# Grouped attention with half of its weights turned in VectorE blocks, values two groups behind, and the first scores of each group pinned in TensorE's order

## The chip, the cores and the metric

The kernel runs on one core of a Trainium2 chip. The metric is the device time of one execution in microseconds (us). Before the change three runs gave 2103.32, 2100.5 and 2106.19 us, so the median is 2103.32 us. All arithmetic is in float32. In the text, PE is TensorE, DVE is VectorE, ACT is ScalarE, POOL is GpSimd, and SP is the engine whose queue issues all DMAs of this kernel.

## What is computed

The reference runs four layers over an input of 8 sequences of 256 tokens with 512 features: a transformer block with rotary attention (8 query heads, one key head) and a gated MLP; a block with cosine attention over 16 heads and a GELU MLP; a grouped attention without MLP; and a layer of 8 small experts. Only the third layer's data path is rewritten by the change, and it computes, cut to what matters:

```python
B, T = 8, 256                     # 16 query heads of 32, 4 key/value heads
h = layernorm(x) * (1.0 + scale) + shift
q = h @ Wq.T                      # 16 heads
c_kv = h @ Wkd.T                  # a latent of 128
k, v = c_kv @ Wku.T, c_kv @ Wvu.T # 4 heads each
q, k = rotary(q), rotary(k)
scores = q @ k.T / sqrt(32)       # 4 query heads share a key head
scores = where(mask, -inf, scores) # window, global keys, no later block of 128
attn = softmax(scores)
x = x + (attn @ v) @ Wo.T
```

The mask hides the second block of 128 keys from the first 128 queries. So one head has 128x128 scores for its first query tile and 128x256 for its second, 384 columns in all.

## The kernel before

**The stages.** `run` (line 1835) calls them in order: attention of layer 0 ("attention0"), its MLP, attention of layer 1 ("attention1"), its MLP, attention of layer 2 ("attention2"), and the experts. The three attentions share one function, `attend` (line 653). By the trace attention2 runs from 1673.9 us to about 1951 us of the span.

**A tile scheduler sets the order.** The Python code lists instructions in program order, and a scheduler then orders each engine's queue: an instruction whose inputs are ready may be put ahead of earlier ones. `keep_in_program_order(ins)` forbids that for one instruction: it stays behind whatever was listed before it on its engine. On the chip each engine then works through its own queue strictly in order and waits on semaphores.

**Groups.** `attend` walks over 8 batches b and, in attention2, 4 groups g of 4 heads. One step of its loop does the following:

- `scored` (line 681): 16 PE passes per group write the scores of 4 heads into 4 PSUM banks "A" (line 693). The heads sit in different row groups of 32 of the array.
- `turned` (line 765) for the group before: PE transposes of the softmax weights, in 128x128 blocks, three per head in attention2, into a bank "C" (line 770), and then a copy back over the weights (lines 478 on DVE and 481 on ACT, by turns). Half of the heads are turned ahead of the softmax, the other half after a share of filler.
- `softmax` (line 699): for each head and query tile, DVE adds the mask and takes the minimum (line 731), then ACT takes the exponential and its sum (line 735). DVE then takes reciprocals of the sums (line 746) and turns them (line 750); two small DMAs through DRAM ("spread", lines 753 and 758) bring them back as a full tile.
- `some(quantum)`: a share of filler from a queue of generators, such as the next batch's projections (`project2`, line 634) and the output product of the batch before (`added`, line 1289). Both use line 629 on PE.
- `weighted` (line 777) and `divided` (line 807) for the group before: 16 PE passes (line 795) multiply the turned weights with the values, and DVE multiplies by the reciprocals (line 812).

**The other path for weights.** `in_blocks` (line 538) says how many of the four heads of a group avoid the PE transposes: two for batches 1 to 6 of attention0 and 0 to 6 of attention1, none in attention2. For such heads the scores and the mask are laid out in blocks, DVE transposes a whole tile of two heads in 32x32 blocks (line 740), four DMAs write it to DRAM ("flip", line 547, in `put`), and one DMA brings it back in place (line 744). Together this is a full transpose with no PE pass. In attention1 that tile is 128x1024.

**The next input.** `prepare` (line 517) normalises the input of batch b+2, transposes it on DVE (line 532) and writes it out in 4 DMAs ("turn", line 547); `fetch` (line 551) reads it back in 8 DMAs (line 565). `modulate` (line 581) then scales its four chunks of features, two on DVE (line 488) and two on ACT (line 489), all pinned in program order at the end of a batch. The first products of the next `project2` read these chunks one by one.

**Rotary part.** In `project2` DVE rotates queries and keys (lines 647 and 648), POOL adds the halves (lines 1651 and 1656), and PE transposes the result (lines 1237 and 1243), which `scored` needs for group 0 of the next batch.

**Buffers.** The pool "p" has 4 buffers for weights, "ctxT" has 4 for finished outputs, "row" has 3, and "wbig" has 8 tiles of 128x2048, of which attention2 uses three.

Of the kernel before, what the change touches and what calls it, by code (L numbers as in the profile page):

```python
# [34 lines left out]
P = 128  # L35
# [62 lines left out]
def constants():  # L98

    f32 = np.float32  # L100
    freqs = (f32(1.0) / f32(10000.0) ** (np.arange(0, 32, 2, dtype=f32) / f32(32))).astype(f32)
    ang = np.arange(S, dtype=f32)[:, None] * freqs[None, :]
    cos = np.cos(ang.astype(np.float64)).astype(f32)
    sin = np.sin(ang.astype(np.float64)).astype(f32)
    rope = np.stack([np.concatenate([cos, cos], 1), np.concatenate([-sin, sin], 1)], 1)
    rope = rope.reshape(TB, P, 2, 32).transpose(1, 0, 2, 3)
    i, k = np.arange(S)[:, None], np.arange(S)[None, :]
    hidden = ((np.abs(k - i) > 64) & (k % 64 != 0)) | (k // P > i // P)
    mask = np.where(hidden, f32(MASKED), f32(0.0))
    mask = np.concatenate([mask[:P, :P], mask[P:, :]], 1)  # L110
    return {
        "inv_freq": np.array([INV_FREQ], f32),
        "rope2": np.ascontiguousarray(rope),
        "mask2": np.ascontiguousarray(mask),
    }


# [61 lines left out]
class Program:  # L179
# [357 lines left out]

    def in_blocks(self, name, b):

        first = {"attention0": 1, "attention1": 0, "attention2": B}[name]  # L540
        return 2 if first <= b < B - 1 else 0

    def put(self, kept, tile):
# [107 lines left out]


    def attend(self, name, n_groups, hd, project, value, finish, work, key_tiles=(2, 2), biased=None,
               extra=None, then=None, spare=None, inverse=None, after=None):

# [23 lines left out]
        def scored(b, g):  # L681
            lhs_rhs = [got[b][0](g, j) for j in range(4)]
            s = [self.bank("A") for _ in range(4)]
            rows = P // hd
            for j0 in range(0, 4, rows):
                for q in range(TB):
                    for j in range(j0, j0 + rows):
                        lhsT, rhs = lhs_rhs[j]
                        keys = rhs(wide[q])
                        if j < self.in_blocks(name, b):  # L690

                            keys = keys.rearrange("p (k c i) -> p c k i", c=4, i=32)
                        nc.tensor.matmul(  # L693
                            s[j][:, at[q] : at[q] + wide[q]], lhsT(q), keys,
                            start=True, stop=True,
                        )
            return s

        def softmax(s, b):
            n_blocks = self.in_blocks(name, b)  # L700
            tot = self.t([P, 4, TB], "tot", 3)
            lows = self.t([P, 4, TB], "low", 3)

            blocks = self.t([P, 8 * P], "p")[:, : 2 * total]
            if n_blocks:
                put = blocks.rearrange("p (c h x) -> p h c x", c=4, h=2)
                ps = []
            else:
                ps = [blocks[:, j * total : (j + 1) * total] for j in range(2)]
            plain = self.t([P, 2, 512], "p")  # L710
            ps += [plain[:, j, :total] for j in range(2)]
            for j in range(4):
                low = lows[:, j, :]
                if biased is None:
                    nc.vector.tensor_reduce(
                        low, s[j].rearrange("p (q k) -> p q k", q=TB), AX.X, ALU.max, negate=True
                    )
                for q in range(TB):
                    cols = slice(at[q], at[q] + wide[q])
                    src, sign, out = s[j][:, cols], 1.0, None  # L720
                    if j >= n_blocks:
                        out = ps[j - n_blocks][:, cols]
                    else:
                        out = put[:, j, :, at[q] // 4 : (at[q] + wide[q]) // 4]
                        src = src.rearrange("p (c x) -> p c x", c=4)
                    if biased is not None:
                        by = biased[j < n_blocks][:, cols]
                        if j < n_blocks:
                            by = by.rearrange("p (c x) -> p c x", c=4)

                        nc.vector.tensor_tensor_reduce(  # L731
                            out, src, by, -1.0, BIG, ALU.add, ALU.min, low[:, q : q + 1]
                        )
                        src, sign = out, -1.0
                    nc.scalar.activation(  # L735
                        out, src, AF.Exp, bias=low[:, q : q + 1], scale=sign,
                        accum_out=tot[:, j, q : q + 1],
                    )
                if j == 3 and n_blocks:
                    nc.vector.transpose(blocks, blocks)  # L740
                    kept = self.flips[self.n_flip % 4][:, : 2 * total]
                    self.n_flip += 1
                    self.put(kept, blocks)
                    nc.sync.dma_start(blocks, kept)
            inv = self.inv[self.n_spread % 2]
            nc.vector.reciprocal(
                inv[:, 0 : 4 * TB].rearrange("p (j q) -> p j q", q=TB), tot
            )
            inv_t = self.t([P, 32], "invT", 2)
            nc.vector.transpose(inv_t, inv)  # L750

            kept = self.spread[self.n_spread % 4]
            nc.sync.dma_start(kept.rearrange("c (b r) -> b c r", b=4), inv_t)
            rows = kept.rearrange("(j q) t -> j (q t)", q=TB)
            by = []
            for c in range(nch):
                t = inverse[(self.n_spread * nch + c) % 4]
                nc.sync.dma_start(
                    t, rows[c * per : (c + 1) * per, :].unsqueeze(1).to_broadcast([per, hd, S])
                )  # L760
                by.append(t)
            self.n_spread += 1
            return (blocks, ps), by
# [43 lines left out]
        def divided(b, o, by):  # L807
            for c in range(nch):
                chunks = ctx.setdefault(b, [])
                out = spare()[len(chunks)] if b == late else self.t([P, S], "ctxT")  # L810
                in_ = o[:, c * S : (c + 1) * S]
                nc.vector.tensor_tensor(out, in_, by[c], ALU.mult)  # L812
                chunks.append(out)
# [2 lines left out]
            chunks = ctx.pop(b)  # L816
            return finish(b, lambda k, t: chunks[k][:, t * P : (t + 1) * P])

        last, steps, done = None, [], []
        for i in range(B * n_groups + 1):  # L820
            ahead = None
            if i < B * n_groups:
# [18 lines left out]
                    turned(j + len(weights) % 4 // 2, p)  # L841
            if ahead is not None:
                ahead = (b, g, softmax(ahead[2], b))
                if g == 0 and ahead_of:
                    for c in (1, 2) if b == 0 else (b + 2,):
                        if c < B:
                            steps.append(self.prepare(name, c, quick=c == 1))
                        elif c == B and after is not None:
                            steps.append(self.prepare(after, 0))
                elif g == 0 and b == B - 1:  # L850
                    steps.append(self.prepare(after, 0))
# [25 lines left out]
                self.end = end  # L877
            else:
                self.some(quantum)
                b, g, (pT, by) = last  # L880
                weights = pT[1]
                for j, p in enumerate(weights[len(weights) // 2 :]):
                    turned(j + len(weights) % 4 // 2, p)
                self.some(quantum)
                divided(b, weighted(b, g, pT), by)
                if g == n_groups - 1:
                    if b != late:
                        self.queue.insert(0, outcome(b))
                    got.pop(b)
                self.some(quantum)  # L890
            if ahead is not None and ahead[1] == n_groups - 1:
                self.modulate()
# [726 lines left out]
    def load_layer2(self):  # L1619
# [5 lines left out]
        self.w2 = w  # L1625
        self.w2o = self.t([P, KC, D], "wo", pool=self.wop)
        self.load(self.w2o, "wo2T")
        rope = self.bank("row")[:, 0 : TB * 64].rearrange("p (t c s e) -> p t c s e", t=TB, c=2, s=2)
        nc.sync.dma_start(rope.rearrange("p t c s e -> p t c (s e)"), d["rope2"])
        self.rope2 = rope  # L1630
        self.mask = self.bank("row")[:, :384]
        nc.sync.dma_start(self.mask, d["mask2"])

    def project2(self, b, got):
        nc, w = self.nc, self.w2
# [38 lines left out]
    def layer2(self):  # L1674
# [2 lines left out]
        self.attend(  # L1677
            "attention2", 4, 32, self.project2, lambda v, g, j, k: v[:, k, j * 32 : (j + 1) * 32],
            lambda b, ctxT: self.added(b, ctxT, self.w2o), (10.4, 6.8), key_tiles=(1, 2),
            biased=(self.mask,), extra={7: (self.expert_inputs(0), 1.74)},  # L1680
            spare=lambda: [spare[:, i, :] for i in range(4)],
            inverse=[spare[:, i, :] for i in range(4, 8)],
        )


# [178 lines left out]
```

## Time and profile before

| what | value |
|---|---|
| median of the runs shown | 2103.32 us |
| the profiled execution's own time | 2104.93 us |
| its span, first to last instruction | 2102.8 us |
| mean granted TensorE clock | 0.989 |
| DVE busy in the span | 1349.8 us (64%) |
| ACT busy in the span | 744.9 us (35%) |
| POOL busy in the span | 303.5 us (14%) |
| attention2, 1673 to 1950 us: PE / DVE / ACT busy | 259.84 / 196.84 / 158.48 us |
| attention1, 920 to 1230 us: PE / DVE / ACT busy | 306.07 / 213.93 / 188.41 us |
| line 770 in attention2: PE busy, passes | 56.59 us, 384 |
| line 770 in attention1: PE busy, passes | 34.35 us, 224 |
| line 740 in attention1: DVE busy, instructions | 34.84 us, 28 |

The page of a profile has one execution. "Busy" of PE counts modelled ends of pipelined passes, so a stretch with little idle time is not yet a stretch at the peak of the array. A fp32 product counts as two passes, a transpose as one. The views by line give busy time and mean duration; the timeline gives starts, so the distance from one start to the next is what a group of passes takes from PE's time.

### The profile page before, as it was taken

The page shows a single profiled execution, that of the slowest core. Times are in us where ns is not written, and L with a number is a line of the kernel's source. Part 1 is how long each engine was busy: PE and PEld are TensorE (multiplying, and loading weights), DVE is VectorE, ACT ScalarE, POOL GpSimd, SP SyncE. Part 2 cuts the span into 40 slices and gives each one's busy share as a digit, 9 for nine tenths or more (in the row PEclk, how much of TensorE's full clock was granted, in tenths as well). Part 3 has the DMA queues.
Part 4 walks back from the last instruction along what each step waited for, and adds up shares of the span by engine and source line. Part 5 has one row for each costly group of instructions (what it writes and reads, how often), then busy time and mean ns, then how long its engine had stood idle before and what let it go on. Part 6 is the DMA issues. An engine that isn't in the chain of part 4 may idle for free.

```text
span 2102.8 us, 36232 instructions
## 1 busy us (share of the span) xinstructions
PE 2043.5 (97%) x12962; PEld 1493.4 (71%) x12962; DVE 1349.8 (64%) x4434; ACT 744.9 (35%) x2330; POOL 303.5 (14%) x340
## 2 busy tenths in 40 slices
PE   7999999999999999999999999999999999999999
PEld 4555569999999999854544448999999755555443
DVE  6767756665675555756676676767666767676233
ACT  3333421111111111146566652222222255556543
POOL 1111200000000000054445621000000111010220
PEclk9999999999999999999999999999999999999999
DMA  8533351112130000335455542234111311210001
GB/s 303 161 113 94 112 202 39 63 51 64 55 114 26 17 31 16 97 95 140 131 144 143 149 134 85 88 100 146 63 46 36 92 42 38 58 38 21 9 36 40
DMA packets 201219, 180.38 MB, mean 86 GB/s; under 512 B 81040, under 2 KB 168016, under 8 KB 201040
## 3 DMA queue, kind: packets, MB, share of 16 engines
q1 hardware_dynamic: 201040, 178.07, 28.5%
q8 instruction: 103, 1.69, 0.3%
q14 instruction: 76, 0.62, 0.1%
HBM read 121.11 MB, written 56.92 MB: 85 GB/s over the span
## 4 chain that ended last, share of the span: by engine, by line
PE 82%; ACT 6%; DVE 6%; DMA 3%; POOL 2%; issue 1%; SPq 0%; ACTq 0%; DVEq 0%; POOLq 0%
PE C L1003 28%; PE C L629 21%; PE A L1052 18%; ACT p L735 4%; PE A L693 4%; PE C L795 4%; PE C L770 3%; PE A L1732 1%; PE C L1751 1%; ACT p L481 1%; DVE p L731 1%; DVE st L448 1%; POOL ss L1479 1%; DVE n L648 1%; DVE qk L647 0%
## 5 line engine op out<-in xcount | busy, mean ns | idle before, releaser
L1003 PE MATMUL C<-hT,wbig 128*128 128x128 f32 x3072 | 416.2, 275 | 0.0
L1003 PEld LDWEIGHTS C<-hT,wbig 128*128 128x128 f32 x3072 | 388.7, 192 | 9.0 <-issue 2.4
L629 PE MATMUL C<-wqkv,hT 128*128 128x512 f32 (+1 forms) x768 | 314.0, 550 | 0.5 <-ACT v L1491 0.4
L735 ACT ACTIVATE p<-p,low 128x256 f32<-128x256 f32 (+1 forms) x512 | 240.0, 471 | 164.8 <-DVE low L731 148.3
L1052 PE MATMUL A<-wbig,p 128*128 128x256 f32 x1024 | 242.2, 379 | 0.0
L629 PEld LDWEIGHTS C<-wqkv,hT 128*128 128x128 f32 x768 | 131.7, 193 | 122.1 <-issue 108.2
L1052 PEld LDWEIGHTS A<-wbig,p 128*128 128x128 f32 x1024 | 189.7, 190 | 23.1
L1033 DVE TENSOR_TENSOR p<-p,C 128x256 f32<-128x256 f32 x192 | 78.9, 418 | 164.2 <-PE C L1003 162.3
L1023 ACT COPY p<-C 128x128 f32<-128x128 f32 x192 | 51.2, 267 | 370.7 <-PE C L1003 362.2
L629 PE MATMUL C<-wo,ctxT 128*128 128x512 f32 x336 | 161.0, 613 | 4.3 <-DVE ctxT L812 4.3
L1003 PE MATMUL C<-ctxT,wbig 128*128 128x128 f32 x1152 | 160.0, 275 | 0.0
L1003 PE MATMUL C<-qk,wbig 128*128 128x128 f32 x1152 | 159.8, 275 | 0.0
L456 POOL TENSOR_SCALAR r<-mv 128x2 f32<-128x2 f32 (+1 forms) x28 | 7.1, 253 | 966.6 <-DVE mv L449 966.6
L731 DVE CUSTOM_DVE_ANT_0 p<-A,row 128x256 f32<-128x256 f32 (+1 forms) x400 | 127.8, 376 | 25.7 <-PE A L693 24.9
L1003 PEld LDWEIGHTS C<-ctxT,wbig 128*128 128x128 f32 x1152 | 144.1, 192 | 0.0
L1003 PEld LDWEIGHTS C<-qk,wbig 128*128 128x128 f32 x1152 | 144.0, 192 | 0.0
L770 PEld LDWEIGHTS C<-ident,p 128*128 128x128 f32 x832 | 96.0, 144 | 67.4 <-issue 37.7
L770 PE MATMUL C<-ident,p 128*128 128x128 f32 x832 | 126.9, 285 | 6.9 <-ACT p L735 2.9
L1375 ACT ACTIVATE p<-C 128x128 f32<-128x128 f32 x64 | 17.8, 278 | 303.2 <-DVE p L1033 303.2
L1024 DVE TENSOR_TENSOR p<-p,C 128x128 f32<-128x128 f32 x192 | 54.5, 284 | 98.3 <-ACT p L1023 98.0
L629 PEld LDWEIGHTS C<-wo,ctxT 128*128 128x128 f32 x336 | 60.0, 193 | 69.9 <-issue 55.9
L735 ACT ACTIVATION_READ_ACCUMULATOR p<-p,low 128x1 f32 x512 | 96.3, 188 | 0.0
(227 smaller groups left out, 3231.5 us busy)
## 6 DMA issues: line engine op xcount, KB each, us to landing
flip<-p SPq DMA_DIRECT2D x160, 128.0 KB
p<-flip SPq DMA_DIRECT2D x40, 512.0 KB
turn<-hT SPq DMA_DIRECT2D x120, 128.0 KB
hT<-turn SPq DMA_DIRECT2D x16, 512.0 KB
kept<-hT SPq DMA_DIRECT2D x16, 512.0 KB
hT<-kept SPq DMA_DIRECT2D x16, 512.0 KB
wbig<-spread SPq DMA_DIRECT2D x64, 128.0 KB
hT<-turn SPq DMA_DIRECT2D x112, 64.0 KB
```

The lines of the kernel that those rows point to most:

```text
L448: nc.vector.bn_stats(st, x)
L629: self.nc.tensor.matmul(out, lhsT(k), rhs(k), start=(k == 0), stop=(k == n - 1))
L693: nc.tensor.matmul(s[j][:, at[q] : at[q] + wide[q]], lhsT(q), keys, start=True, stop=True,)
L731: nc.vector.tensor_tensor_reduce(out, src, by, -1.0, BIG, ALU.add, ALU.min, low[:, q : q + 1])
L735: nc.scalar.activation(out, src, AF.Exp, bias=low[:, q : q + 1], scale=sign, accum_out=tot[:, j, q : q + 1],)
L770: nc.tensor.transpose(m[:, n * P : (n + 1) * P], p[:, at[q] + k * P : at[q] + (k + 1) * P], self.ident,)
L795: mm = nc.tensor.matmul(o[i * hd : (i + 1) * hd, c * S + q0 * P : (c + 1) * S], value(got[b][1], g, j, k), weights(j, mine), start=(k == 0 ...
L1003: nc.tensor.matmul(m[:, c : c + P], w[:, k * P : (k + 1) * P], b[:, k], start=(first and k == 0), stop=(k == steps - 1), skip_group_check= ...
L1023: nc.scalar.copy(g[:, 0, :], m[:, 0:P])
L1024: nc.vector.tensor_tensor(g[:, 0, :], g[:, 0, :], m[:, P : 2 * P], ALU.add)
L1033: nc.vector.tensor_tensor(g[:, 1:3, :], g[:, 0, :].unsqueeze(1).to_broadcast([P, 2, P]), m[:, 2 * P : 4 * P].rearrange("p (i t) -> p i t", ...
L1052: nc.tensor.matmul(acc[at][:, half * S : (half + 1) * S], left, right, start=(p == 0 and half == 0), stop=(p == 3), skip_group_check=True,)
```

## The change

In attention2 two of the four heads of a group take the path through DVE blocks and DMAs in batches 0 to 6 (batch 7 stays as it was). In those batches the values of a group are computed two steps after its scores, no longer one. The weights move from the pool "p" to four tiles of "wbig" (`rooms`), and the outputs from "ctxT" to a fifth (`contexts`). The mask is loaded a second time, in blocks. In all three attentions the first score product of every group is pinned behind what PE was given before it in program order.

```diff
+        "mask2_blocks": np.concatenate([mask[:, :P], in_blocks(mask[:, P:])], 1),
...
-        first = {"attention0": 1, "attention1": 0, "attention2": B}[name]
+        first = {"attention0": 1, "attention1": 0, "attention2": 0}[name]
         return 2 if first <= b < B - 1 else 0
...
-                        nc.tensor.matmul(
+                        mm = nc.tensor.matmul(
                             s[j][:, at[q] : at[q] + wide[q]], lhsT(q), keys,
                             start=True, stop=True,
                         )
+
+                        if j == q == 0:
+                            self.tc.keep_in_program_order(mm)
...
-            blocks = self.t([P, 8 * P], "p")[:, : 2 * total]
+            if rooms is None:
+                blocks, plain = self.t([P, 8 * P], "p"), self.t([P, 2, 512], "p")
+            else:
+                room = rooms[self.n_spread % 4]
+                blocks, plain = room[:, : 8 * P], room[:, 8 * P :]
+                plain = plain.rearrange("p (j x) -> p j x", j=2)
+            blocks = blocks[:, : 2 * total]
...
-                out = spare()[len(chunks)] if b == late else self.t([P, S], "ctxT")
+                if b == late:
+                    out = spare()[len(chunks)]
+                elif contexts is not None:
+                    out = contexts[:, b % 2 * 4 + len(chunks), :]
+                else:
+                    out = self.t([P, S], "ctxT")
...
+                lag = 2 if rooms is not None and self.in_blocks(name, b) else 1
+                due.append((i + lag, *ahead))
...
-                b, g, (pT, by) = last
-                weights = pT[1]
+                weights = last[2][0][1]
                 for j, p in enumerate(weights[len(weights) // 2 :]):
                     turned(j + len(weights) % 4 // 2, p)
                 self.some(quantum)
-                divided(b, weighted(b, g, pT), by)
-                if g == n_groups - 1:
-                    if b != late:
-                        self.queue.insert(0, outcome(b))
-                    got.pop(b)
+                while due and due[0][0] <= i:
+                    _, b, g, (pT, by) = due.pop(0)
+                    divided(b, weighted(b, g, pT), by)
+                    if g == n_groups - 1:
+                        if b != late:
+                            self.queue.insert(0, outcome(b))
+                        got.pop(b)
...
-        rope = self.bank("row")[:, 0 : TB * 64].rearrange("p (t c s e) -> p t c s e", t=TB, c=2, s=2)
+        both = self.bank("row")
+        rope = both[:, 0 : TB * 64].rearrange("p (t c s e) -> p t c s e", t=TB, c=2, s=2)
...
-        self.mask = self.bank("row")[:, :384]
+        self.mask = both[:, TB * 64 :]
         nc.sync.dma_start(self.mask, d["mask2"])
+        self.mask_blocks = self.bank("row")[:, :384]
+        nc.sync.dma_start(self.mask_blocks, d["mask2_blocks"])
...
-            biased=(self.mask,), extra={7: (self.expert_inputs(0), 1.74)},
+            biased=(self.mask, self.mask_blocks), extra={7: (self.expert_inputs(0), 1.74)},
...
+            rooms=[self.t([P, 4 * 512], "wbig") for _ in range(4)],
+            contexts=self.t([P, 8, S], "wbig"),
```

More of the change, by code (lines that the diff above doesn't have):

```diff
@@ L653, in attend @@
     def attend(self, name, n_groups, hd, project, value, finish, work, key_tiles=(2, 2), biased=None,
-               extra=None, then=None, spare=None, inverse=None, after=None):
+               extra=None, then=None, spare=None, inverse=None, after=None, rooms=None, contexts=None):
         late = B - 3
@@ L709, in softmax @@
                 ps = [blocks[:, j * total : (j + 1) * total] for j in range(2)]
-            plain = self.t([P, 2, 512], "p")
             ps += [plain[:, j, :total] for j in range(2)]
@@ L817, in outcome @@
             return finish(b, lambda k, t: chunks[k][:, t * P : (t + 1) * P])
-        last, steps, done = None, [], []
+        last, steps, done, due = None, [], [], []
         for i in range(B * n_groups + 1):
```

## The prediction

> **What bounds the kernel now.** I read the page first, then the busy time by window, the timeline of PE in attention2, and last the waits.
>
> ```profile
> span 2102.8 us, 36232 instructions
> PE 2043.5 (97%) x12962; PEld 1493.4 (71%) x12962; DVE 1349.8 (64%) x4434; ACT 744.9 (35%) x2330; POOL 303.5 (14%) x340
> ...
> L770 PE MATMUL C<-ident,p 128*128 128x128 f32 x832 | 126.9, 285 | 6.9 <-ACT p L735 2.9
> ```
>
> PE is busy 97% of the span, so time can be won only where PE gets less to do or stops waiting. The transposes of line 770 are one such item. Next, one batch of attention2 (the pattern repeats every 34.43 us):
>
> ```profile
> 1749.40:1783.90 34.50, 32.95 (x232) 18.07 (x231) 25.43 (x115) 19.61 (x78) 4.32 (x6) 1.00 0.22 49
> ```
>
> The columns are PE, PE weight loads, DVE, ACT and POOL. PE idles 1.55 us of it; DVE has 9 us to spare and ACT 15. The timeline of PE in that batch (start, duration, line, passes, wait ahead):
>
> ```profile
> 1752.23 1.36 PE L795 MATMUL C<-p,v 128*32 128x256 f32 x16
> 1753.53 1.98 PE L629 MATMUL C<-wo,ctxT 128*128 128x512 f32 x4
> ...
> 1756.31 0.87 PE L770 MATMUL C<-ident,p 128*128 128x128 f32 x6
> 1757.02 1.88 PE L629 MATMUL C<-wo,ctxT 128*128 128x512 f32 x4
> ...
> 1776.30 0.63 PE L795 MATMUL C<-p,kT 128*32 128x256 f32 x6
> 1777.46 0.84 PE L795 MATMUL C<-p,kT 128*32 128x256 f32 x10 [0.53 <-ACT p L481]
> 1778.23 0.66 PE L1237 MATMUL C<-ident,qk 128*128 128x128 f32 x4
> 1778.72 0.27 PE L1243 MATMUL C<-ident,kr 128*128 128x128 f32 x1
> 1779.73 0.66 PE L1237 MATMUL C<-ident,qk 128*128 128x128 f32 x4 [0.73 <-POOL qk L1651]
> ```
>
> Six transposes take 0.71 us from start to next start. The 16 value passes take 0.79 us when nothing holds them (twice in this batch), but 1.30 and 1.93 us in these two sets: they follow at once on the copy of the weights just turned. The waits of PE's weight loads over five batches (from 1715 us; total, times, longest) say the same:
>
> ```profile
> PEld C L795 <- ACT p L481: 10.4, 14, 1.0
> PEld C L1237 <- POOL qk L1651: 4.9, 5, 1.0
> ```
>
> **The change, part by part.** *Transposes.* Seven batches x 4 groups x 2 heads x 3 = 168 passes leave PE. Start to start they cost 0.71/6 = 0.118 us, so 19.7 us. By busy time of the group in attention2 (56.59 us for 384, 0.147 each, with pipelined ends) it is 24.8 us. I take 19.7.
>
> The Trainium skill, "VectorE: DVE Perf Modes", sections "The three transpose paths" and "Rules for kernel authors", speaks against the edit: a 128x128 transpose belongs on TensorE, since VectorE only turns 32x32 blocks. It gives 390 ns for one on TensorE (bf16); 168 of those would be 65.5 us, more than the trace has for all 384, so the trace decides.
>
> *DVE and ACT.* Without PE transposes 28 x 2 copies of 128x384 leave DVE (median 552 ns): -30.9 us. ACT keeps 64 of its copies, since both plain heads' copies fall to it. 28 block transposes of 128x768 come. Their nearest row is that of 128x1024:
>
> ```profile
> L740 DVE STREAM_TRANSPOSE p<-p x40: 1226/1245/1247, 81.6 to 1217.5; 128x1024 f32<-128x1024 f32 x40
> ```
>
> Scaled by columns that is 0.93 us, +26.1 us in all; unscaled it is 34.9. DVE ends near where it was, hidden under PE. The block layouts cost nothing: in attention1 line 731 takes 419 ns in blocks and 420 plain, lines 735, 693 and 795 likewise show one duration for both.
>
> *DMAs.* Per group four puts and a fetch, 140 more on SP. In attention1:
>
> ```profile
> 1056.84 1.76 SPq L547 DMA_DIRECT2D flip<-p x4
> 1058.70 0.53 SPq L753 DMA_DIRECT2D spread<-invT x1
> ...
> 1060.52 0.34 SPq L744 DMA_DIRECT2D p<-flip x1
> ```
>
> That is 2.1 us of issue per group in a step of some 7.5 us, and about 2 us between puts and fetch. In the built queue a group's fetch often stands behind the first puts of the next group, so it waits for that group's DVE transpose. At the tightest (group 0) the fetch is issued 5.7 us after the scores of group 1 begin (4.5 until that transpose ends, 1.2 for two puts and the fetch), and the values run 13.7 us after them (a step of 8.5 and 5.2 of the next): 8.0 us for the landing. Attention1 ran with 8.8 us (fetch 1050.26, values 1059.09) and lost 0.5 us to flips in 240 us. I take no wait; the last rival has the other end. The second mask, one load of about 192 KB as the first, comes during the MLP. The "wbig" rooms free up with that MLP's last products, and the first mask additions stand behind those in any case: nothing.
>
> *Values two groups behind.* They no longer follow a fresh copy: 1.30 + 1.93 - 2 x 0.79 = 1.65 us a batch, six batches, -9.9 us; 0 at worst.
>
> *What is late next.* In the built order the output product goes behind the next projections, so the queries' rotation is done early and the 0.73 us wait on POOL goes, with 0.25 us on the query copy (0.98 a batch). The last key rotation is now tight. After the scores of group 3 start, PE reaches its transpose in 0.87 + 0.35 + 1.72 + 0.35 + 0.49 + 0.79 + 1.2 = 5.8 us. DVE, behind that group's softmax (exponentials end at 5.3), does the reciprocals and the rest of the rotation in five steps of 0.2 us, POOL adds in 0.46: 6.8. The key's copy then stands behind others on DVE for some 0.6 us more. So 1.6 us for 0.98: +0.6 x 6 = +3.7 us, bounds -5.9 (no wait at all) and +6.
>
> *The next input is the main price.* On SP the eight loads of line 565 (0.62 us each) now stand behind the first flip puts of group 3, where before they came two groups earlier. In the built queues of DVE and ACT the scaling (lines 488 and 489; 0.40 and 0.59 us) moves into or behind the softmax of the next group 0, and PE's first projection products wait for it. PE reaches them 0.87 (scores) + 0.35 (three transposes) = 1.2 us after those scores start. From the timelines DVE starts on scores 0.95 us after PE, ACT at 1.35, four exponentials take 1.78 us, so eight end at 5.0. In two batches (those loading for batches 4 and 6) DVE scales after the reciprocals: first chunk at 5.0 + 0.3 + 0.4 = 5.7, a stall of 4.5 us. In three (batches 3, 5, 7) it does after four of the mask additions: 0.95 + 1.12 + 0.4 = 2.5, a stall of 1.3, and 0.45 more for the last chunk. Batch 2's stands ahead of them: none. Sum 2 x 4.5 + 3 x 1.75 = +14.2 us; if the loads' landing is the limit, all five cost 4.5: +22; if PE's other waits cover it, 0.
>
> *Starts and pins.* Batch 0 of attention2 takes 39.0 us for less work than a later batch, so the softmax chain sets it; of its 2.8 us I count 1.8 as not won. In attention0 the first score that ran ahead filled a PE wait (two passes at 206.67, then a 1.07 us wait before values at 208.44); pinned, the wait grows by what the scores lose: 16 passes together take 2.00 us, the other 14 alone 1.99. So 0 there. Around 63 to 75 us eight score products are joined that ran in three pieces: -1 us, bounds -3 and +2.
>
> *Sum.* -19.7 - 9.9 + 3.7 + 14.2 + 1.8 - 1 = -10.9 us, so 2094.0 against the profiled execution's 2104.93 (2102.8 and 2.1 around the span). That execution lies 1.6 us over the median of 2103.32, so a median of 2092.
>
> **Rivals.** *The stalls on the next input don't happen* or are covered, because the loads land early and the engines reach the scaling sooner than I count. For it: DVE and ACT have room, and PE takes the chunks one by one between other products. Against it: engine queues are strict, and the scaling stands behind the exponentials. Without the 14.2 and 3.7 it is 2103.3 - 19.7 - 9.9 + 0.8 = 2074.5.
>
> *The chain takes it all back.* Group steps shrink from 8.6 us to 6 in the second half of a batch, and a group's chain of scores, additions, exponentials and reciprocals takes 5.7. With all five stalls at 4.5 us and half of the gain at the values it is -19.7 - 5 + 22 + 3.7 + 0.8 = +1.8, so 2105.
>
> *Slower: the flips land late.* Place: the value products, 28 groups. Price: whatever the landing takes over 8.0 us. The rows leave it between 2 us and 8.8. At 8.8 PE waits 0.8 x 28 = 22 us, which gives 2092 + 22 = 2114. From 0.4 us late (landing 8.4) the gain is gone, and from 0.65 it is slower by 0.3%. For it: SP's queue is in order, a fetch stands behind another group's transpose, and a delayed group delays the next. Against it: other groups have more room than group 0.
>
> **How the numbers follow.** The forecast, 2092 with its own range of 2084 to 2097, gets 0.58; no stalls 0.14; taken back 0.10; late flips 0.18. A measurement here can't tell less than 0.3% (6.3 us) from no change. So faster (under 2097) 0.72, within 0.10, slower 0.18. The range is 2074 to 2110: it leaves out the lower part of the second case and the upper half of the last.
>
> **What would show it.** Line 770 with 664 passes in all; line 740 with 68; no waits of line 795 on line 481 in batches 1 to 6 of attention2; new waits of line 629 on lines 488 and 489 at the head of each batch, 4 to 5 us in two; a period alternating between about 32 and 35 us; attention0, attention1 and the MLPs within 2 us. I am wrong if value products wait on flips, if the period stays over 34.4 us, or if the first stages move by more.

## The result and the profile after

The changed kernel takes 2106.48 us (median; 2103.71 to 2114.49), the kernel before beside it 2103.17 us (2099.64 to 2106.19). The ratio is 1.002 with a 95% interval of 1.0012 to 1.0027: slower by 3.3 us or 0.2%, where 11.3 us less had been forecast. The top of the changed kernel's page, span and busy time:

```profile
span 2103.1 us, 36173 instructions
PE 2008.4 (95%) x12794; PEld 1469.5 (70%) x12794; DVE 1351.3 (64%) x4406; ACT 745.2 (35%) x2330; POOL 305.0 (15%) x340
```

The span was 2102.8 us. PE has 168 passes and 35 us of busy time less, as the change meant, and the span is no shorter. PE waits that much longer. Where it does so is seen from distances inside each profile (starts of PE instructions, us), since the way to the key transpose near 132 us varies from one profile to the next (128.4 to 134.2 us over all kernels here):

| stretch | before | after | difference |
|---|---|---|---|
| attention0: from the key transpose after a 1.16 us wait near 132 us to the first product of its MLP | 151.0 | 156.7 | +5.7 |
| attention1: first scores to last values | 345.8 | 348.0 | +2.2 |
| attention2: first scores to last values | 276.3 | 268.0 | -8.3 |

So by these two profiles the change won 8.3 us in the stage that it is for, and lost 7.9 us in two stages where only the pin touches anything. Their spans differ by 0.3 us where the medians differ by 3.3: the execution shown before took 1.8 us more than its kernel's median, the one after 1.3 us less. Attention2 after, by batches: the columns are a batch's window, its length, the busy time of PE, PE weight loads, DVE, ACT and POOL, the granted clock of PE, and the DMA share and GB/s.

```profile
1747.44:1779.71 32.27, 29.66 (x207) 15.14 (x206) 25.68 (x110) 19.62 (x78) 4.63 (x6) 1.00 0.54 141
1779.71:1816.66 36.95, 30.92 (x208) 16.31 (x207) 25.82 (x108) 19.85 (x78) 3.70 (x4) 0.91 0.54 136
1816.66:1848.91 32.25, 29.49 (x207) 15.22 (x206) 25.52 (x108) 19.74 (x78) 3.70 (x4) 1.00 0.58 145
1848.91:1884.35 35.44, 30.26 (x207) 16.09 (x206) 22.82 (x105) 19.83 (x78) 3.47 (x4) 0.95 0.57 144
```

Each of these batches took 34.43 us before. Two are now at 32.3, the other two at 37.0 and 35.4, with a clock under 1. PE's timeline at the head of the second shows why:

```profile
1780.68 0.55 PE L781 MATMUL C<-ident,wbig 128*128 128x128 f32 x3
1785.68 2.90 PE L630 MATMUL C<-hT,wqkv 128*128 128x256 f32 x6 [4.45 <-DVE hT L489]
1788.37 1.91 PE L630 MATMUL C<-wqkv,hT 128*128 128x512 f32 x2
```

The first products of the next projection wait 4.45 us for the scaled input, as forecast. They then run slowly: two passes of 512 columns take 1.91 us, where four take 1.88 elsewhere. The same place by windows, with the clock in the third last column:

```profile
1781.20:1785.68 4.48, 0.03 (x2) 0.03 (x1) 3.57 (x18) 3.99 (x18) 0.00 (x0) 0.74 0.47 73
1785.68:1789.70 4.02, 4.02 (x8) 2.66 (x9) 0.41 (x1) 1.08 (x2) 0.00 (x0) 0.50 0.63 127
1789.70:1794.00 4.30, 4.30 (x25) 1.73 (x23) 0.42 (x1) 0.37 (x1) 0.00 (x0) 0.94 0.78 217
```

After the wait PE is granted half its clock for about 4 us. This wait therefore costs more than its length.

In attention0 the loss is one event in batch 2. DVE's timeline after, with the sums of the MLP's weights (line 926), the turning of the reciprocals, and the multiplication of the output (line 828; 812 before):

```profile
150.46 0.42 DVE L926 TENSOR_TENSOR wbig<-wbig 128x256 f32<-128x256 f32 x1 [2.55 <-DMA wbig<-in_wgT]
150.80 0.20 DVE L761 STREAM_TRANSPOSE invT<-inv 128x32 f32<-128x32 f32 x1
152.83 0.42 DVE L926 TENSOR_TENSOR wbig<-wbig 128x256 f32<-128x256 f32 x1 [1.83 <-DMA wbig<-in_wgT]
...
154.18 0.74 DVE L828 TENSOR_TENSOR ctxT<-C,wqkv 128x256 f32<-128x256 f32 x2
```

and before:

```profile
151.07 0.43 DVE L907 TENSOR_TENSOR wbig<-wbig 128x256 f32<-128x256 f32 x1 [2.27 <-DMA wbig<-in_wgT]
151.48 0.74 DVE L812 TENSOR_TENSOR ctxT<-C,wqkv 128x256 f32<-128x256 f32 x2
```

Before, one wait for the weights' loads stood ahead of the output's multiplication; now two waits and five sums do. The turned reciprocals, which that multiplication needs by way of DRAM, stand behind the first of them. On PE's timeline the output product that follows, after and then before:

```profile
154.65 7.11 PE L630 MATMUL C<-wo,ctxT 128*128 128x512 f32 x12 [3.84 <-DVE ctxT L828]
```

```profile
151.95 5.42 PE L629 MATMUL C<-wo,ctxT 128*128 128x512 f32 x12 [0.89 <-DVE ctxT L812]
```

The wait grew by 2.95 us, and the twelve passes behind it took 1.69 us longer, again at a lowered clock. No program line of these sums was changed. The pin changed when PE's passes fall, and the scheduler, which places what is ready, put the queues of DVE, ACT and SP together in another order (POOL's is as before).

In attention1 the loss sits in the last batch, which has little filler. Before, PE ran the scores of a coming group while weights were on their way through DRAM:

```profile
1227.09 1.80 PE L693 MATMUL A<-kT,qT 32*128 32x256 f32 x16
1229.06 0.63 PE L795 MATMUL C<-p,v 128*32 128x256 f32 x6 [0.17 <-DMA p<-flip]
```

After, the scores have to stay behind those values, and PE waits:

```profile
1234.55 0.63 PE L806 MATMUL C<-p,v 128*32 128x256 f32 x6 [2.00 <-DMA p<-flip]
1235.62 1.05 PE L806 MATMUL C<-p,v 128*32 128x256 f32 x10 [0.43 <-ACT p L482]
...
1238.51 1.15 PE L696 MATMUL A<-kT,qT 32*128 32x256 f32 x16
```

Counted from attention1's first scores, the values keep their distance to those of before up to the end of batch 6 and fall back by 2.4 us around these lines. In the four kernels with pins in attention1 they fall back there by 2.4 to 4.0 us, in the nine others of the experiments by 0.0.

### The profile page after: what moved, and what is told of

It is laid out like the page before. It is cut to its first block, busy times and chain, and to the rows that moved or that the text cites. A ratio compares the mean times of both kernels' runs of the same rounds, so it can differ in the third digit from the quotient of the medians.

```text
span 2103.1 us, 36173 instructions
## 1 busy us (share of the span) xinstructions
PE 2008.4 (95%) x12794; PEld 1469.5 (70%) x12794; DVE 1351.3 (64%) x4406; ACT 745.2 (35%) x2330; POOL 305.0 (15%) x340
## 4 chain that ended last, share of the span: by engine, by line
PE 76%; DVE 9%; ACT 7%; DMA 3%; POOL 2%; issue 2%; SPq 1%; ACTq 0%; DVEq 0%; POOLq 0%
PE C L1022 28%; PE A L1071 18%; PE C L630 18%; ACT p L746 4%; PE A L696 3%; PE C L806 3%; ACT wbig L746 2%; PE C L781 2%; PE A L1756 1%; PE C L1775 1%; DMA hT<-turn 1%; DVE st L449 1%; DVE wbig L742 1%; SPq L566 1%; DVE n L649 1%
## 5 line engine op out<-in xcount | busy, mean ns | idle before, releaser
L746 ACT ACTIVATE p<-p,low 128x256 f32<-128x256 f32 x256 | 126.8, 498 | 71.0 <-DVE low L742 66.5
L746 ACT ACTIVATE wbig<-wbig,low 128x128 f32<-128x128 f32 (+1 forms) x256 | 113.1, 444 | 85.3 <-DVE low L742 82.3
L630 PE MATMUL C<-wo,ctxT 128*128 128x512 f32 x224 | 107.1, 617 | 6.1 <-DVE ctxT L828 5.9
L746 ACT ACTIVATE p<-A,low 128x256 f32<-128x256 f32 x128 | 59.2, 486 | 102.2 <-DVE low L726 102.2
L1498 POOL TENSOR_TENSOR ss<-ss,neg_half 128x16 f32<-128x16 f32 x32 | 93.6, 2925 | 2.7
L742 DVE CUSTOM_DVE_ANT_0 wbig<-A,row 128x128 f32<-128x128 f32 (+1 forms) x256 | 73.9, 352 | 14.9 <-PE A L696 14.8
L630 PEld LDWEIGHTS C<-wo,ctxT 128*128 128x128 f32 x224 | 41.0, 195 | 54.2 <-issue 40.4
```

What stands on the lines that cost most here:

```text
L630: self.nc.tensor.matmul(out, lhsT(k), rhs(k), start=(k == 0), stop=(k == n - 1))
L742: nc.vector.tensor_tensor_reduce(out, src, by, -1.0, BIG, ALU.add, ALU.min, low[:, q : q + 1])
L746: nc.scalar.activation(out, src, AF.Exp, bias=low[:, q : q + 1], scale=sign, accum_out=tot[:, j, q : q + 1],)
L1498: nc.gpsimd.tensor_tensor(r, r, self.neg_half[:, 0:16], ALU.pow)
```

## The experiments

The kernel before ran beside each of them. Its median was 2103.57 us beside the first four below, and 2101.58 or 2101.51 beside the others. Where kernels of the two sets are compared, "counted from before" takes each by its distance from the kernel before beside it; the changed kernel's is +3.3 us.

**The pin alone.**

```diff
-                        nc.tensor.matmul(
+                        mm = nc.tensor.matmul(
...
+                        if j == q == 0:
+                            self.tc.keep_in_program_order(mm)
```

(on the kernel before)

> The kernel before, with nothing but the pin of each group's first score product. Theory (the pins lost what the blocks won): about 8 us slower than before at the head of attention2, 5.4 us of it already at the first product of layer 0's MLP and 2 to 3 us more in the last batch of attention1; attention2 itself between 0 and +3 us; so 2109 to 2114 us. Rival (the pins cost nothing, and the first stages lost time by something else that came with the change, such as the room of the second mask): within 2 us of before, first scores of attention2 at 1673 to 1675 us.

Measured: 2115.27 us, 1.0056 of before (1.0044 to 1.0068). Attention0's stretch is 157.2 us, attention1's 347.8, attention2's 277.1: +6.2, +2.0 and +0.8. In batch 2 of attention0 the output product waits 4.34 us for DVE. The pins cost what the changed kernel lost ahead of attention2, and a little there too. That is 9.0 of the 11.7 us between the medians; where the rest lies isn't shown. The median is 1 us over the theory's range.

**The change without pins.**

```diff
-                        if j == q == 0:
-                            self.tc.keep_in_program_order(mm)
```

> The changed kernel without any pin. Theory: up to the head of attention2 it is the kernel before to within 1 us (first scores of attention2 at 1673 to 1675 us). In attention2 two groups of scores run ahead of the next projections and wait for score banks, which costs about what the wait for the next input cost; so attention2 wins 4 to 9 us and the time is 2094 to 2099 us. Rival (the pins are what makes attention2 faster): attention2 wins nothing and the time is 2102 us or more.

Measured: 2109.0 us, 1.0022 (1.0012 to 1.0032). In the first stages PE's passes have the order of before, as expected. Even so this profile takes 1544.5 us from the key transpose near 131 us to the first scores of attention2, where that of before takes 1541.0. The ten profiles with this order have 1540.8 to 1544.5 us, so executions differ by that much; the four kernels with pins in these stages have 1545.4 to 1551.2. Attention2 isn't that of before: 279.3 us, 3 longer. Here the rival holds. On PE's timeline at the head of a batch, the scores of groups 1 and 2 have been drawn ahead of the projections:

```profile
1776.33 2.49 PE L696 MATMUL A<-v,qT 32*128 32x128 f32 x16 [0.33 <-DVE low L740]
1779.43 0.89 PE L696 MATMUL A<-v,qT 32*128 32x128 f32 x4 [0.61 <-DVE low L740]
1780.48 2.66 PE L696 MATMUL A<-v,qT 32*128 32x128 f32 x12 [0.15 <-DVE low L740]
```

They trickle through as DVE frees score banks, nearly 7 us for what takes twice 0.87 when nothing holds it, and the three batches from 1774 us on take 36.5 to 38.3 us. I had taken this for the same price as the wait that it covers; it is higher. With blocks and a late input, attention2 needs its pin.

**Pins in attention2 alone.**

```diff
-                        if j == q == 0:
+                        if j == q == 0 and name == "attention2":
```

> The changed kernel with pins in attention2 alone. Theory: the first stages are those of before, attention2 is that of the changed kernel, 8.2 us shorter than before; so 2103.2 - 8.2 = 2095 us, range 2093 to 2097. Rival (what attention0 and attention1 lost is given back later in any case, because the loads of the next weights set the start of the stages behind them): 2101 us or more.

Measured: 2095.85 us, 0.9967 (0.9955 to 0.9979). As the theory has it: attention1 is back at 345.7 us, attention2 takes 267.0. That is 10.6 us less than the changed kernel by the medians, where the single profiles of the two differ by 9.5 in span (2093.6 us here). Nothing of the first stages' loss would have come back by itself.

**The input two groups earlier**, on the kernel above:

```diff
                     for _ in step:
-                        if b > 0 and ahead_of:
+                        if b > 0 and ahead_of and (name != "attention2" or g > 0):
                             break
```

> As the run with pins in attention2 alone, and there the next input is normalised and turned wholly in group 0, so that its loads are issued two groups earlier and the scaling stands ahead of the softmax of the next group 0 on DVE and ACT. Theory (the five stalls of 1.2 to 4.5 us are the scaling's place in the queues): the stalls of 12.4 us in sum go, so 2095 - 12 = 2083 us, range 2080 to 2088. Rival (the chain of scores, additions, exponentials and reciprocals sets the group's step, and the stall only covers it): PE waits as long elsewhere, 2092 us or more.

Measured: 2083.09 us, 0.9902 (0.989 to 0.9915). 12.8 us less for 12.4 us of waits on the input: the theory holds. A smaller wait has come up in their place. SP's queue in this kernel, with the eight input loads ahead of the flips of group 2:

```profile
1754.67 5.26 SPq L566 DMA_DIRECT2D hT<-turn  x8
1759.97 1.10 SPq L548 DMA_DIRECT2D flip<-wbig  x2
...
1762.89 0.34 SPq L755 DMA_DIRECT2D wbig<-flip  x1
```

and what PE then does:

```profile
1766.62 1.51 PE L806 MATMUL C<-wbig,kT 128*32 128x256 f32 x16 [3.21 <-DMA wbig<-flip]
```

This is the rival of late flips; in another batch such a wait is 0.5 us.

**The weights' loads held back.** All pins, and the loads behind DVE's sums kept on SP until batch 3 of attention0:

```diff
-                for i in (0, 1, 2, -1, 3, -2, -3, -4):
-                    self.layer0_up(i if i >= 0 else -1 - i, int(i >= 0))
+        def gated_loads():
+            for i in (0, 1, 2, -1, 3, -2, -3, -4):
+                self.layer0_up(i if i >= 0 else -1 - i, int(i >= 0), True)
...
+            if held:
+                self.tc.keep_in_program_order(ins)
```

> The changed kernel with all pins, and the loads of the first MLP's weights held back on SP until batch 3 of attention0, so that DVE's sums of these weights come after batch 2. Theory (the pins lost 5 us of attention0 because DVE stood waiting for these loads with the output's multiplication of batch 2 queued behind): the 3.84 us wait of the output product at 154.65 us goes, attention0 gets 3.5 to 5 us shorter, and the time is 2106.5 - 4 = 2102.5 us, range 2101 to 2104. Rival (attention0 lost by PE's own order, the passes that no longer run ahead): the wait only changes its place and the time stays within 1.5 us of 2106.5 us.

Measured: 2105.75 us, 1.0019 (1.001 to 1.0028). The wait at 154 us is gone, as the theory says, yet attention0's stretch stays at 157.3 us, as the rival says. A new wait stands in batch 3:

```profile
198.07 2.71 PE L806 MATMUL C<-p,kT 128*64 128x256 f32 x16 [3.49 <-DMA p<-flip]
```

On DVE's timeline the sums now run from 178 us to 188.6 with little between them. The maxima of a group (line 726) come at 189.6 and its block transpose at 192.3, so its flip is late. Either way DVE's queue holds a block of work that isn't urgent, ahead of one that is.

**The same loads in four shares**, two tiles of weights at the end of each of batches 1 to 4, pinned on SP like those above:

```diff
+        def gated_loads(n):
+            for i in (0, 1, 2, -1, 3, -2, -3, -4)[2 * n : 2 * n + 2]:
+                self.layer0_up(i if i >= 0 else -1 - i, int(i >= 0), True)
```

> The changed kernel with all pins, and the loads of the first MLP's weights pinned on SP in four shares, two tiles of weights at the end of each of batches 1 to 4 of attention0. Theory (the six to eight loads in one block keep SP for 9 to 10 us; whatever stands behind them, DVE's sums and the output's multiplication in batch 2, or the flips when they were held until batch 3, comes late by it): no PE wait over 2 us between 105 and 290 us, attention0 4 to 6 us shorter than in the changed kernel, the time 2106.5 - 5 = 2101.5 us, range 2100 to 2103. Rival (it is PE's pinned order that loses, wherever the loads are): 2105 to 2107 us as in the run before with the loads held.

Measured: 2100.2 us, 0.9993 (0.9984 to 1.0002), so 6.3 us less than the changed kernel, 4.6 counted from before. Attention0's stretch is 151.4 us, 5.3 less, and no PE wait over 2 us is left in it. In batch 2 sums still stand ahead of the output's multiplication on DVE, but their weights are there, so nothing waits; the output product's passes follow on PE without a wait (two lines of DVE's timeline, then one of PE's):

```profile
147.26 0.20 DVE L761 STREAM_TRANSPOSE invT<-inv 128x32 f32<-128x32 f32 x1
148.87 0.76 DVE L828 TENSOR_TENSOR ctxT<-C,wqkv 128x256 f32<-128x256 f32 x2
148.76 6.28 PE L630 MATMUL C<-wo,ctxT 128*128 128x512 f32 x14
```

Attention1 keeps its loss (348.4 us). So nearly all of attention0's loss comes from the block of loads and sums, in a queue order that the pin brought about, and little from PE's pinned order itself. The kernel before with its loads spread was not run: its own wait at this place is 0.89 us, so it could gain too, and with the 0.4 us by which 151.4 is over 151.0 up to some 1.3 us may be PE's order.

**No blocks, values two behind**, with pins in attention2:

```diff
-        first = {"attention0": 1, "attention1": 0, "attention2": 0}[name]
+        first = {"attention0": 1, "attention1": 0, "attention2": B}[name]
...
-                lag = 2 if rooms is not None and self.in_blocks(name, b) else 1
+                lag = 2 if rooms is not None and b < B - 1 else 1
```

> As the run with pins in attention2 alone (2095.85 us), but with no head in blocks there: all four heads are transposed on PE again, the values stay two groups behind. Theory by the prediction's terms: 19.7 us of transposes come back, the 11 to 12 us of stalls on the next input go with the flips, the 9.9 us at the value products stay won; so 2095.85 + 19.7 - 11.5 = 2104 us if the rest is equal, or 2103.57 - 9.9 = 2094 us counted from before; the two sums differ by what else the blocks cost, so 2094 to 2104. Rival (values two groups behind win nothing, the waits at the copies only move to the transposes' banks): 2104 us or more.

Measured: 2089.79 us, 0.9955 (0.994 to 0.997). This is 6 us faster than the kernel with blocks (2095.85 us), 4 counted from before. Neither sum had seen that: the second, taken from the kernel before beside this run (2101.58 - 9.9 = 2091.7), is 2 us too high.

**The same without pins** (the pin's two lines taken out as above).

> As the run without blocks (2089.8 us), without its pins too, so that only the values two groups behind are left of the change. Theory (without flips the scaling of the next input stands early in its queues, so nothing tempts the order to run two groups of scores ahead): within 2 us of 2089.8 us. Rival (the pins are worth 10 us in attention2 with or without blocks, as the runs without pins, 2109.0 us, and with them in attention2, 2095.85 us, would have it): 2097 us or more.

Measured: 2090.5 us, 0.9949 (0.9932 to 0.9966). By the median the theory holds: without flips the pin isn't needed, and values two groups behind, with the rooms that they need, win some 11 us by themselves. But in the single profiles attention2 takes 267.7 us without pins and 262.5 with them, so whether pins are worth something there stays open.

**Values one group behind**, on the kernel with the earlier input:

```diff
-                lag = 2 if rooms is not None and self.in_blocks(name, b) else 1
+                lag = 1
```

> As the run with the input two groups earlier (2083.1 us), but with values one group behind the scores, so that the weights' way through DRAM has one step less. Theory: from the scores of a group to its fetched weights it takes 8 to 12 us (scores 1759.36, transposed 1763.37, fetch issued 1768.45), and values one step behind run 11 to 13 us after those scores in some groups and 8 in others; PE waits 0.5 to 2 us in each of 28 groups, 2097 to 2140 us. Rival (values one behind only lose the 9.9 us of waits at the copies): 2090 to 2095 us.

Measured: 2112.33 us, 1.0046 (1.0032 to 1.006): 29 us more than with two, 31 counted from before. PE's waits at the value products, in attention2:

```profile
PE C L806 <- DMA wbig<-flip: 20.4, 9, 4.9
PE C L806 <- ACT wbig L482: 6.7, 5, 2.9
```

The second step is what hides the way through DRAM.

**Pins in batches 1 to 6 of attention2 only**, earlier input:

```diff
+                        if j == q == 0 and name == "attention2" and 0 < b < B - 1:
```

> As the run with the input two groups earlier (2083.1 us), with pins in batches 1 to 6 of attention2 only. Theory (a pin pays only where filler from the next projections stands behind it, and costs where the softmax chain sets the step: in batch 0 PE waits 5.71 us for the normalised rows of batch 1, and the last batch of attention1 lost 2.3 us): 1 to 4 us faster, 2079 to 2082 us. Rival (first and last batch are bound by the chain with or without the pin): 2083 us.

Measured: 2084.59 us, 0.9917 (0.9904 to 0.9931), no faster than 2083.09: a miss. In batch 0 PE waits no longer for the normalised rows, but nearly as long for score banks (4.75 us against 5.71), and the batch takes 2.1 us more. The batches behind it take less, so attention2 in the profile is 1.4 us shorter (254.3 against 255.7); the medians don't show it.

**The input loads on POOL or ACT**, earlier input:

```diff
-                    self.nc.sync.dma_start(to[:, k, t], parts[:, k, t])
+                    queue = self.nc.gpsimd if name == "attention2" else self.nc.sync
+                    queue.dma_start(to[:, k, t], parts[:, k, t])
```

(and `self.nc.scalar` in the second)

> As the run with the input two groups earlier (2083.1 us), with the eight loads of the next input issued by POOL instead of SP. Theory (these loads keep SP for 5.3 us, the flips of group 2 behind them land late, 3.2 us of PE wait in one batch): the waits of the value products on flips go and the period falls from 31.8 to 31 us or less, 2077 to 2081 us. Rival (POOL waits for the turned input to be written, and the additions of the rotary part stand behind that): 2084 to 2092 us.

Measured: 2078.26 us, 0.9892 (0.9877 to 0.9907), the fastest version of all, 28 us under the changed kernel (27 counted from before) and 4.8 under the kernel with these loads on SP (2.8 counted from before). One wait of a value product on a flip is left, of 1.38 us.

> The same with ACT issuing the eight loads. Theory (SP's time is what matters, ACT has 15 us to spare in a batch): 2077 to 2082 us. Rival (ACT waits for the written input and issues for some us while exponentials stand behind it): slower than 2083.1 us, up to 2100 us.

Measured: 2086.65 us, 0.9926 (0.9912 to 0.994); 3.6 us slower than with the loads on SP (5.6 counted from before). ACT has time to spare, but exponentials stand behind the loads there: PE's transposes wait 4.6 us for them in attention2, as the rival has it. POOL's line of the eight loads:

```profile
1755.77 5.98 POOL L567 DMA_DIRECT2D hT<-turn  x8
```

The Trainium skill, "DMA: Bandwidth & Descriptors", section "Issuing engine by pattern", names SP for simple loads and calls its path generally faster. The eight loads do take longer on POOL, 5.98 against 5.26 us. The kernel is faster even so: SP's queue, where the flips stand, is free of them, and the 3.21 us wait on a flip is gone.

Attention2 without blocks and with them, the loads on POOL, three batches each (columns as above):

```profile
1739.29:1772.33 33.04, 31.48 (x231) 17.68 (x230) 25.94 (x114) 19.40 (x78) 4.62 (x6) 1.00 0.23 52
1772.33:1805.38 33.05, 31.49 (x231) 17.68 (x231) 25.81 (x112) 19.40 (x78) 3.69 (x4) 1.00 0.23 51
1805.38:1838.43 33.05, 31.49 (x232) 17.69 (x231) 25.81 (x112) 19.40 (x78) 3.69 (x4) 1.00 0.23 51
```

```profile
1738.33:1768.84 30.51, 28.41 (x208) 15.23 (x207) 25.78 (x111) 19.11 (x78) 10.57 (x14) 1.00 0.54 153
1768.84:1799.38 30.54, 28.63 (x207) 15.16 (x206) 25.42 (x108) 19.69 (x78) 9.67 (x12) 1.00 0.61 172
1799.38:1829.74 30.36, 28.63 (x207) 15.17 (x206) 25.47 (x108) 19.57 (x78) 9.57 (x12) 1.00 0.60 158
```

Where nothing else interferes, 24 transposes fewer make a batch 2.5 to 2.7 us shorter, 0.11 us each. The price by starts that the prediction took, 0.118, was near it.

## Why the prediction was wrong

The step that failed is *Starts and pins*: "pinned, the wait grows by what the scores lose ... So 0 there", and in all -1 us with bounds of -3 and +2. The pins cost 7.9 us outside attention2 by the profiles, and 10.6 us by the medians of the kernel with and without them there (11.0 counted from before). Counted so the account closes: with pins in attention2 alone the kernel is 7.7 us under the one before, where -9.9 had been summed for attention2, and the pins elsewhere add 11.0, where -1 had been summed. That is 2.2 and 12.0 of the 14.2 us between -10.9 and +3.3. The step asked only what PE's own passes lose by staying in order, and for attention0 that answer was nearly right. It left out that the orders of DVE's, ACT's and SP's queues are built around PE's, so that a block of loads and sums which the change doesn't touch could come to stand ahead of an urgent multiplication. It also left out the last batch of attention1, where scores run ahead while the values wait for DRAM: there the kernels with pins lose 2.4 to 4.0 us, and those without nothing. The reason is read from the trace; no run took the pin out of that batch alone. The -1 us around 63 to 75 us can't be seen, since the profiles vary by more than that up to the key transpose. "Attention0, attention1 and the MLPs within 2 us" was named as a sign of error, and it was this one that came.

Within attention2 the sum was -9.9 us with the batch that isn't won, and the profile has -8.3. The terms, by the lengths of attention2 in the profiles (276.3 us before):

| term | forecast | measured | from |
|---|---|---|---|
| values two behind, with pins | -9.9 | -13.8 | no blocks, pins: 262.5 |
| transposes, with batch 0 not won | -17.9 | -13.5 | loads on POOL: 249.0 |
| flips behind the input's loads on SP | 0 | +6.7 | loads on SP, early: 255.7 |
| late input | +14.2 | +11.3 | late: 267.0 |
| last key rotation | +3.7 | 0 | 0.98 us of waits a batch, as before |

These are differences of single profiles, so a microsecond or two in them means little. They add up to -9.3; the changed kernel has 1.0 us more than the kernel with pins in attention2 alone, 268.0.

- *Values.* Right in mechanism: in a steady batch the period falls from 34.43 to 33.05 us, 1.38 a batch where 1.65 was counted. More comes from the first batches, which I hadn't counted (39.0 to 35.3 us in batch 0), and in part from the pins: without them attention2 takes 267.7, only 8.6 us less than before. By the medians the values are worth 11 to 12 us with or without pins. That no wait of the value products on the copies would be left was wrong: 1.8 us in four of them, now on ACT, which does all the copies.
- *Transposes.* The price of a pass nearly held (168 x 0.118 is 19.8 us, not the 19.7 of the sum). The -13.5 also has in it what the early loads on POOL are worth, which no run without blocks shows. In batches 0 and 1 nearly nothing came of it (67.0 us together against 67.5). I read the chain of the softmax and the way of the input as what sets the pace there, which no run tested, and had counted that for batch 0 alone. The Trainium skill's rule that a 128x128 transpose belongs on TensorE ("VectorE: DVE Perf Modes", "Rules for kernel authors"), weighed in the prediction, has this case with it as the blocks were put in: with the input behind their flips they cost more than they saved (2095.85 against 2089.79 us). It has the case against it once the input's loads are early and on POOL (2078.26).
- *The next input.* The forecast stalls of 4.5 us stand at 4.45 in the two batches named, and the three smaller ones at 1.17 where 1.3 was counted. 12.4 us of waits in sum, and 12.8 us gone when they were taken away. The lowered clock after the two long ones was not in the sum.
- *Last key rotation.* 0.46, 0.27 and 0.25 us a batch, the sum that it had before, not 1.6: mis-sized.
- *Flips.* No value product waited on a flip in the changed kernel, so this rival did not decide it. It appears once the stalls that gave the flips time are gone.

Of the rivals none named a slower kernel by the pin. The time of "the chain takes it all back", 2105, is near, but for another reason: attention2 kept its gain. That 2106.48 lies inside the range of 2074 to 2110 is luck for the same reason: no case in it has the price of the pins.

## What to carry to other kernels

A constraint on one engine's order, put in for one stage, should be limited to that stage: the queues of other engines are built around it, and work that isn't urgent can come to stand ahead of work that is, far from the edit. Cost a change in every stage that runs the edited function, with the built order of DVE's and SP's queues beside PE's. A round trip through DRAM that is hidden by one more step of lag competes for its issuing queue with every other transfer there, so move or advance these first. And try the parts apart: here the values two groups behind were worth more than the whole change.

## What the runs showed of the hardware

Long waits are followed by a lowered clock of PE. After waits of 4.45 us and 3.84 us the granted clock was 0.50 over the next 4.0 us and 0.58 over the next 3.4; the wait of 3.49 us with the held loads was followed by 0.63 over 3.9 us, and that of 3.21 us with the early input by 0.65 over 4.4. In the batches of attention2 whose longest wait was 1.17 us it stayed at 1.00. Length alone doesn't decide it: a wait of 2.12 us at 1846.92 us, with values one behind, was followed by 0.61 over 4.0 us, and one of 3.42 us at 67.59 us, with the held loads, by 1.00 over 3.9. The batch at 1779.71 us is 4.7 us longer than its neighbours for 3.3 us more of waiting, so the lowered clock took about 1.4 us. The one at 1848.91 us has the same wait, but PE is busy only 0.7 us longer in it, and it is 3.2 us longer in all. The Trainium skill, "TensorE: Matmul & The Clock Gate", in the part on the HAM clock gate, says that an idle window of some 3.4 us halves the clock and that a busy one of the same length restores it; the three waits above that length agree, but waits of 3.21 and 2.12 us lowered it too, and that of 3.42 us didn't. A forecast stall of such a length should be priced with it: by PE's busy time the two of 4.45 us here would have added some 2 us to the sum.
